# Layer 0's last query frequencies: two token groups in one call on eighths of TensorE

## The chip, the cores and the metric

One NeuronCore of a Trainium2 chip runs the whole network in one launch. The metric is the device time of the program in microseconds (us), the median of the runs shown. Engine names follow the profile: PE is TensorE's matmuls, PEld its weight loads, DVE is VectorE, ACT ScalarE, POOL GpSimd, SP the engine that issues most DMAs.

## The reference, cut to what matters

Four layers, each a gated cross-attention followed by a gated feed-forward part, on 4 x 256 tokens of width 256 with a context of 4 x 64 rows of width 64. The change concerns the cross-attention of layer 0 alone:

```python
q_hk = (hidden_q @ Wq.T).reshape(Bv, Sv, H, K)           # 16 heads
q_big = jnp.einsum('bshk,hkq->bshq', q_hk, w_kc_q)       # 192 values a head
q_big = _apply_rope(q_big, sin_q, cos_q)                 # rotation by position
kv_r = _apply_rope(kv_c, sin_k, cos_k)
q_r = jnp.einsum('bshq,hqr->bhsr', q_big, W_qr)
k_r = jnp.einsum('bld,hdr->bhlr', kv_r, W_kr)
scores = jnp.einsum('bhsr,bhlr->bhsl', q_r, k_r)
attn = jax.nn.softmax(scores, axis=-1)
ctx_c = jnp.einsum('bhsl,bld->bhsd', attn, kv_r)
```

The kernel folds `w_kc_q` into `Wq` and `W_kr` into `W_qr`, so that each head's rotated query of 192 values is multiplied by one matrix of 192 x 64 to the "latent" query of 64 values, which meets the rotated context directly. The rotation couples value q with value q + 96: a head has 96 frequencies, each with two sides.

## The kernel before, in words

The 1024 tokens are 8 tiles of 128 or two groups g of 512 (NG = 2). The 16 heads are taken four at a time, f = 0 to 3 (NQ = 4). Inside f, the heads are split by `up` (rows 0 to 63 or 64 to 127 of the partitions) and i (two heads in each half).

attention0 (L629 to L722) works on 24 rotations, step n. `rotated(n)` (L639) multiplies the folded query weights `weff0` with the transposed, normalised tokens xT[g] into a "wide" PSUM tile of 128 x 2 x 512 (s = 0, 1 are the two sides; each takes two accumulating matmuls through the helper on L389), multiplies it by the cosine and sine tables on VectorE (L650) and adds up on GpSimd (L658, L659). The result, `qr` or a slot of the ring `rotated`, holds for k = 0 and 1 the first 64 frequencies of head i = k, and for k = 2 the last 32 frequencies of both heads i of each half: four quarters of 32 rows, one head in each.

Steps before: unit u = 2 f + g, k = 0, 1, 2, so n = 3 u + k. `to_latent(u)` (L662, matmuls on L671) takes the results of k = 0 and 1 to latents: contraction over 64 rows, 64 output columns, accumulated over s in two PSUM tiles `mm` (one for each `up`), head i in the half of partitions 64 i to 64 i + 63. `rest_to_latent(u)` (L679, matmuls on L685) adds the result of k = 2: contraction over 64 rows that hold two heads, against a weight `rest` of 64 x 128 that is zero where a row's head is not the column's head. GpSimd sets `rest` to zero first (L457), and fold_scores0 (L450; matmuls on L470 and L484) fills the non-zero blocks. Then ScalarE copies both tiles into `qcT[g]` (L687).

What sets the order: each engine runs its own stream, and the loop on L693 places the calls: to_latent(u - 1) in step 3 u, rest_to_latent(u - 1) in step 3 u + 1, fold_queries0 for the next f (L504, matmuls on L516) in every sixth step, a piece of fold_output (L546) in four late steps, small preparations (`later`) from step 6. The layer norm of the second group and its transposes (L374) are called in step 1. The buffers: PSUM has four `mm` and two `wide` tiles; the SBUF pool `t4` has six slots, from which every rotation takes two (rope0, rope1) and every odd one a third (qr); even ones use the ring of two.

latent_attend (L578) follows. `values(b)` (matmuls on L591) makes the folded output weights for batch b, with index j for the head's half; `scores(t)` (L609) multiplies `qcT` with the block-diagonal context `bd_k`, whose two halves of rows are the two heads; softmax, transposes and the output product (L624) come behind. Groups are batches: g = 1 is b >= 2.

Of the kernel before, what the change touches and what calls it, by code (L numbers as in the profile page):

```python
# [38 lines left out]
B, S, D = 4, 256, 256  # L39
# [3 lines left out]
NG = T // TH  # L43
TPG = TH // P
L, DC = 64, 64
NH, DK, CQ, CQH, R = 16, 128, 192, 96, 64
NP = NH // 2
NQ = NH // 4
# [35 lines left out]
def tile_flamingo(ctx: ExitStack, tc: tile.TileContext, a: dict, out: bass.AP):  # L84
# [7 lines left out]
    def ps_mm():  # L92
        return psum.tile([P, 512], F32, tag="mm", name="mm", bufs=4)
# [356 lines left out]
    def fold_scores0():  # L450

        wqk = region("wqk", 2048, "wqk0")
        wide = wqk[:, :1024].rearrange("p (f i s d) -> p f i s d", f=NQ, i=2, s=2)
        rest = wqk[:, 1024:].rearrange("p (f s i d) -> p f s i d", f=NQ, s=2, i=2)
        nc.gpsimd.memset(rest, 0.0)  # L457
        rT = w_rk0[:, : NP * CQ].rearrange("r (h q) -> r h q", h=NP)
        kT = w_rk0[:, NP * CQ :].rearrange("r (h d) -> r h d", h=NP)
        for f2 in range(NQ // 2):  # L460
            wides = [ps_mm() for _ in range(2)]
            rests = [ps_mm() for _ in range(2)]
            for f in range(2):
                for i in range(2):
                    for s in range(2):
                        h = (f2 * 2 + f) * 2 + i
                        for up in range(2):
                            rows = slice(up * R, (up + 1) * R)
                            at_ = ((f * 2 + i) * 2 + s) * DC
                            nc.tensor.matmul(  # L470
                                wides[up][rows, at_ : at_ + DC],
                                rT[rows, h, s * 64 : (s + 1) * 64],
                                kT[rows, h, :],
                                start=True,
                                stop=True,
                            )
            for f in range(2):
                for i in range(2):
                    for s in range(2):
                        h = (f2 * 2 + f) * 2 + i  # L480
                        for up in range(2):
                            rows = slice(up * R, (up + 1) * R)
                            lo, at_ = up * R + i * 32, (f * 2 + s) * DC
                            nc.tensor.matmul(  # L484
                                rests[up][lo : lo + 32, at_ : at_ + DC],
                                rT[rows, h, 128 + s * 32 : 128 + (s + 1) * 32],
                                kT[rows, h, :],
                                start=True,
                                stop=True,
                                tile_position=(up * R, lo),  # L490
                            )
            fs = slice(f2 * 2, f2 * 2 + 2)
            for up in range(2):
                rows = slice(up * R, (up + 1) * R)
                evacuate(wide[rows, fs].rearrange("p f i s d -> p (f i s d)"), wides[up][rows])
                for i in range(2):
                    rows = slice(up * R + i * 32, up * R + (i + 1) * 32)
                    evacuate(
                        rest[rows, fs, :, i, :],
                        rests[up][rows, :256].rearrange("p (f s d) -> p f s d", f=2, s=2),  # L500
                    )
        return wide, rest.rearrange("p f s i d -> p f s (i d)")

    def fold_queries0(f):  # L504

# [69 lines left out]
        t = big[:, HALF:].rearrange("p (g r t) -> p g r t", g=NG, r=NP)  # L575
        return [t[:, g] for g in range(NG)]

    def latent_attend(qcT, wvo, gate):  # L578


        vos: dict = {}

        def values(b):

            v = region(("wqk", "weff")[b % 2], 2048, "vo").rearrange("p (q j o) -> p q j o", q=4, j=2)
            for r in range(2):
                pss = [ps_mm() for _ in range(2)]
                for a_ in range(2):
                    for j, ps in enumerate(pss):
                        rows = slice(j * DC, (j + 1) * DC)  # L590
                        nc.tensor.matmul(  # L591
                            ps[a_ * L : (a_ + 1) * L, :],
                            bd_k[rows, b, j * L : (j + 1) * L],
                            wvo[rows, 4 * r + a_ : 4 * r + a_ + 3 : 2, :],
                            start=True,
                            stop=True,
                        )
                for j, ps in enumerate(pss):
                    evacuate(v[:, 2 * r : 2 * r + 2, j, :], ps.rearrange("p (q o) -> p q o", q=2))
            vos[b] = v.rearrange("p q j o -> p (q j) o")  # L600

        def scores(t):
            g, i = divmod(t, TPG)
            if t % 2 == 0:
                values(t // 2)
            ps = ps_wide()
            for pr in range(NP):
                q, a_ = divmod(pr, 2)
                nc.tensor.matmul(  # L609
                    ps[:, q // 2, q % 2 * 256 : (q % 2 + 1) * 256].rearrange("p (j a l) -> p j a l", j=2, a=2)[:, :, a_, :],  # L610
                    qcT[g][:, pr, i * P : (i + 1) * P],
                    bd_k[:, t // 2, :],
                    start=True,
                    stop=True,
                )
            e = t4([P, NH, L], "attn")
            exponentials(e, ps.rearrange("p a (h l) -> p (a h) l", l=L))
            return e

        def attend(t, e):  # L620
            aT, vo = transposed_pairs(e), vos[t // 2]
            ps = ps_mm()
            for s in range(NP):
                nc.tensor.matmul(ps[:, :D], aT[:, s, :], vo[:, s, :], start=(s == 0), stop=(s == NP - 1))  # L624
            return ps

        in_flight(scores, attend, gate)

    def attention0(gate):  # L629

        xT = [transposed(layernorm(0))]
        fold_queries0(0)
        qcT = latents()
        ring = region("weff", 2048, "rotated").rearrange("p (i s t) -> p i s t", i=2, s=2)
        units = [(f, g) for f in range(NQ) for g in range(NG)]
        made: dict = {}
        sums: dict = {}

        def rotated(n):  # L639
            u, k = divmod(n, 3)  # L640
            f, g = units[u]
            ps = ps_wide()
            for s in range(2):
                mm2(ps[:, s, :], lambda c: weff0[:, c, f, 2 * k + s, :], xT[g])
# [14 lines left out]
            nc.gpsimd.tensor_tensor(qr[:, 1, :], halves[1][:, 0, :], halves[1][:, 1, :], ALU.add)  # L659
            made[n] = qr  # L660

        def to_latent(u):  # L662

            f, _ = units[u]
            pss = sums[u] = [ps_mm() for _ in range(2)]
            qrs = [made.pop(3 * u + i) for i in range(2)]
            for s in range(2):
                for i in range(2):
                    for up in range(2):
                        rows = slice(up * 64, (up + 1) * 64)  # L670
                        nc.tensor.matmul(  # L671
                            pss[up][i * DC : (i + 1) * DC, :],
                            wide[rows, f, i, s, :],
                            qrs[i][rows, s, :],
                            start=(s == 0),
                            stop=False,
                        )

        def rest_to_latent(u):  # L679
            f, g = units[u]  # L680
            pss, qr = sums.pop(u), made.pop(3 * u + 2)
            for s in range(2):
                for up in range(2):
                    rows = slice(up * 64, (up + 1) * 64)
                    nc.tensor.matmul(pss[up], rest[rows, f, s, :], qr[rows, s, :], start=False, stop=(s == 1))  # L685
            for up in range(2):
                last.append(nc.scalar.copy(qcT[g][:, 2 * f + up, :], pss[up]))  # L687

        wide = None
        later = prepare()  # L690
        last: list = []
        output = fold_output(w_kv0, [lambda: (w_o0, NH, lambda: None)])
        for n in range(3 * len(units) + 2):  # L693
            u, k = divmod(n, 3)
            if n == 1:
                xT.append(transposed(layernorm(1)))
            if u < len(units):
                rotated(n)
                if k == 1 and u % 2 == 0 and u // 2 + 1 < NQ:
                    fold_queries0(u // 2 + 1)  # L700
                if k == 1 and u >= len(units) - 4:
                    next(output)
            if wide is None:
                wide, rest = fold_scores0()
            if k == 0 and u >= 1:
                to_latent(u - 1)
            if k == 1 and u >= 1:
                rest_to_latent(u - 1)
            if n >= 6:
                next(later, None)  # L710
        tanh = nc.scalar.activation(tg, gates, AF.Tanh)
# [6 lines left out]
        wvo = at_once(output)  # L718
        for e in (0, 4, 8):
            load_experts0(e, e + 4)  # L720
        latent_attend(qcT, wvo, gate)
        load_experts0(12, 16)  # L722

    def fold1():
# [1030 lines left out]
```

## Time and profile before

| | us |
|---|---|
| median of 3 runs | 988.71 (983.85 to 992.39) |
| the profiled execution | 982.89 |
| its span, first to last instruction | 980.9 |
| PE busy in the span | 872.9 (4451 matmul records) |
| DVE, ACT, POOL busy | 531.6, 274.3, 300.0 |
| L389, 192 records | 88.8 |
| L671, 128 records in two groups | 15.5 and 15.5 |
| L685, 64 records in two groups | 8.2 and 7.9 |

A page of the profile shows, for one execution, groups of instructions: line, engine, operation, the names of what is written and read, the shape ("64*128" on PE: contraction rows by weight columns), the count, then busy time and mean ns of one, then the idle time of the engine just before them with what ended it. A group's busy time counts overlapped instructions once, so count times mean can be more. Other views give the chain of work that ended last in order of time, the busy time of all engines in a stretch, and who waited for whom. All times are from the span's start.

### The profile page before, as it was taken

What the parts mean: (1) busy time and instruction counts of PE and PEld (TensorE: products, weight loads), DVE (VectorE), ACT (ScalarE), POOL (GpSimd) and SP (SyncE); (2) the same over time, 40 slices, a digit from 0 to 9 for tenths busy, and PEclk for the clock granted to TensorE, in tenths of its full rate; (3) what the DMA queues carried; (4) which work ended last, traced back from release to release, by engine and by line L of the source; (5) the groups of instructions that cost most, each with busy time, mean ns of one, the idle gap of its engine ahead of it and who ended that gap; (6) DMA issues with size and microseconds to landing.
All of it is one profiled execution on the core that took longest, in us unless ns stands there. A gap on an engine that the chain in (4) does not pass through costs nothing.

```text
span 980.9 us, 12657 instructions
## 1 busy us (share of the span) xinstructions
PE 872.9 (89%) x4451; PEld 569.9 (58%) x4453; DVE 531.6 (54%) x1185; ACT 274.3 (28%) x531; POOL 300.0 (31%) x259
## 2 busy tenths in 40 slices
PE   5999998999899999997899978979638899999992
PEld 3544335876678866774547854746424556666661
DVE  4656455756953344552627749958785855222213
ACT  2211013334123232331223447034303532122220
POOL 1445451310065665751003128003101402133220
PEclk9999999999989999997999999979858989999997
DMA  9200017300154444225730000530000011011004
GB/s 351 84 15 11 28 36 230 89 22 22 33 153 160 131 152 151 90 69 157 260 115 1 1 1 27 189 116 2 22 0 1 1 44 33 22 48 39 29 16 140
DMA packets 35481, 75.82 MB, mean 77 GB/s; under 512 B 4551, under 2 KB 22207, under 8 KB 34106
## 3 DMA queue, kind: packets, MB, share of 16 engines
q1 hardware_dynamic: 27834, 56.22, 17.1%
q0 software_dynamic: 7296, 18.50, 6.1%
q8 instruction: 39, 0.64, 0.3%
q10 hardware_dynamic: 288, 0.26, 0.1%
q14 instruction: 24, 0.20, 0.1%
HBM read 63.42 MB, written 12.98 MB: 78 GB/s over the span
## 4 chain that ended last, share of the span: by engine, by line
PE 53%; DVE 17%; issue 14%; DMA 8%; POOL 4%; ACT 4%; SPq 0%; POOLq 0%; DVEq 0%; ACTq 0%
PE wide L389 9%; PE wide L1158 5%; PE mm L624 5%; DMA zz<-ring,scratch 4%; PE mm L1193 3%; PE wide L1400 3%; PE mm L419 2%; PE mm L1532 2%; POOL zz L1205 2%; PE mm L389 2%; PE wide L609 2%; PE mm L685 1%; PE mm L1421 1%; PE mm L897 1%; PE mm L671 1%
## 5 line engine op out<-in xcount | busy, mean ns | idle before, releaser
L405 POOL TENSOR_TENSOR attn<-attn,sm 128x1024 f32<-128x1024 f32 x32 | 60.8, 1900 | 235.1 <-DVE sm L404 163.1
L1178 DVE TENSOR_TENSOR blk<-wide,blk 128x176 f32<-128x176 f32 (+1 forms) x75 | 32.5, 433 | 142.0 <-ACT blk L1177 142.0
L650 DVE TENSOR_TENSOR rope<-wide,big 128x512 f32<-128x512 f32 x96 | 59.6, 683 | 57.1 <-PE wide L389 55.6
L389 PE MATMUL wide<-xT,big 128*128 128x512 f32 x192 | 88.8, 610 | 0.3 <-ACT big L524 0.3
L1129 POOL DMA_INDIRECT xs<-xd,big x55 | 55.3, 1005 | 70.3 <-DVE shared L1310 34.5
L1158 PE MATMUL wide<-big,blk 128*128 x220 | 74.1, 458 | 0.0
L1169 PE MATMUL wide<-big,blk 128*128 x160 | 72.2, 593 | 0.5 <-DVE blk L1143 0.5
L1205 POOL DMA_INDIRECT zz<-ring,big x55 | 56.1, 1021 | 31.9 <-DVE ring L1202 11.2
L389 PEld LDWEIGHTS wide<-xT,big 128*128 128x128 f32 x192 | 35.7, 193 | 48.7 <-issue 38.7
L1177 ACT ACTIVATE blk<-wide 128x176 f32<-128x176 f32 (+1 forms) x75 | 29.4, 392 | 122.8 <-PE wide L1158 61.6
L624 PE MATMUL mm<-vo,attnT 128*128 128x256 f32 x256 | 60.4, 390 | 0.9 <-ACT attnT L420 0.9
L1193 PE MATMUL mm<-big,blk 88*128 x220 | 56.8, 379 | 0.5 <-ACT blk L1186 0.5
L624 PEld LDWEIGHTS mm<-vo,attnT 128*128 128x128 f32 x256 | 48.4, 194 | 9.5 <-ACT attnT L420 3.3
L420 ACT COPY attnT<-mm 128x512 f32<-128x512 f32 x64 | 35.0, 588 | 65.0 <-PE mm L419 65.0
L374 PE MATMUL mm<-ident,xn 128*128 128x128 f32 x112 | 24.3, 363 | 30.3 <-DVE xn L362 18.0
L1193 PEld LDWEIGHTS mm<-big,blk 88*128 88x128 f32 x220 | 41.4, 189 | 15.5 <-ACT blk L1186 1.4
L1158 PEld LDWEIGHTS wide<-big,blk 128*128 128x128 f32 x220 | 39.5, 190 | 12.5
L403 DVE TENSOR_REDUCE sm<-attn 128x16 f32<-128x1024 f32 x32 | 38.9, 1215 | 14.5 <-ACT attn L397 12.3
L419 PE MATMUL mm<-ident,attn 128*128 128x128 f32 x256 | 36.3, 289 | 10.8 <-POOL attn L405 10.8
L1169 PEld LDWEIGHTS wide<-big,blk 128*128 128x128 f32 x160 | 28.8, 190 | 28.9 <-issue 28.2
L424 DVE SCALAR_TENSOR_TENSOR x<-mm,tg,x 128x256 f32<-128x256 f32 x48 | 22.9, 476 | 39.8 <-PE mm L624 19.7
L1129 POOL DMA_INDIRECT xs<-xd,scratch x20 | 19.2, 961 | 81.5 <-PE mm L1141 59.5
(334 smaller groups left out, 1702.4 us busy)
## 6 DMA issues: line engine op xcount, KB each, us to landing
big<-in_L_w_gate_up SPq DMA_DIRECT2D x8, 1024.0 KB, 8.2
zt<-zz SPq DMA_DIRECT2D x16, 384.0 KB, 5.1
big<-in_L_w SPq DMA_DIRECT2D x4, 1408.0 KB, 6.8
big<-in_L_w_down SPq DMA_DIRECT2D x8, 512.0 KB, 11.9
w_L_qk<-in_L_qk SPq DMA_DIRECT2D x4, 896.0 KB, 8.6
big<-in_L_w SPq DMA_DIRECT2D x4, 704.0 KB
big<-in_L_wo SPq DMA_DIRECT2D x1, 2048.0 KB, 12.8
xd<-xn SPq DMA_DIRECT2D x16, 128.0 KB, 1.8
```

Of the source, the lines that this page charges most:

```text
L389: nc.tensor.matmul(ps, w(c), xT[:, c, :], start=(c == 0), stop=(c == 1))
L403: nc.vector.tensor_reduce(sm, e, AX.X, ALU.add)
L405: nc.gpsimd.tensor_tensor(e, e, sm.unsqueeze(2).to_broadcast([P, groups, n]), ALU.mult)
L419: nc.tensor.transpose(ps[:, i * P : (i + 1) * P], ev[:, pr * P : (pr + 1) * P], ident)
L420: nc.scalar.copy(aT[:, half * 4 : half * 4 + 4, :].rearrange("p i t -> p (i t)"), ps)
L624: nc.tensor.matmul(ps[:, :D], aT[:, s, :], vo[:, s, :], start=(s == 0), stop=(s == NP - 1))
L650: nc.vector.tensor_tensor(m[:, s, :].rearrange("q (b t) -> q b t", t=S), ps[:, s, :].rearrange("q (b t) -> q b t", t=S), table, ALU.mult,)
L1129: nc.gpsimd.indirect_dma_start(out=xs, out_offset=None, in_=self.xd, in_offset=bass.IndirectOffsetOnAxis(ap=self.gather[:, b : b + 1].bitc ...
L1158: nc.tensor.matmul(ps[:, 0, : 2 * n], st[:, c * P : (c + 1) * P], self.w[:, bass.ds(r + c * 2 * n, 2 * n)], start=False, stop=(c == 1),)
L1169: nc.tensor.matmul(ps[:, k, :n], st[:, c * P : (c + 1) * P], self.w[:, bass.ds(r + (2 * c + k) * n, n)], start=(c == 0), stop=(c == 1),)
L1193: nc.tensor.matmul(ps[:, :D], hT[:, j * P : (j + 1) * P], self.w[: self.chunk, bass.ds(r + j * D, D)], start=(j == 0), stop=(j == self.n - 1),
L1205: s = nc.gpsimd.indirect_dma_start(out=self.z, out_offset=bass.IndirectOffsetOnAxis(ap=self.scatter[:, b : b + 1].bitcast(U32), axis=0), i ...
```

## The change

- `rest` loses its zero blocks and the memset: a weight of 32 rows by 64 columns for each quarter of rows.
- The order of rotations inside f becomes (k, g) = (0,0), (1,0), (2,0), (2,1), (0,1), (1,1), so that the two results of k = 2 stand side by side; n = 6 f + m.
- `rest_to_latent(f)` is called once for each f, in its sixth step, for both groups: 16 matmuls on tiles of 32 x 64 with a written tile position. For g = 0 it closes the sums that to_latent(f, 0) opened in the fourth step; for g = 1 it opens them, and to_latent(f, 1) closes them in the second step of the next f.
- For g = 1 the two heads of a pair lie in swapped halves (`half = i ^ g`), and values() for batches 2 and 3 stores its output with j swapped to match.
- `finished` does the copies of L687, two for each f and g as before.
- The layer norm and transposes of the second group are called in step 2 in place of step 1.

```diff
@@ -453,8 +453,7 @@

         wqk = region("wqk", 2048, "wqk0")
         wide = wqk[:, :1024].rearrange("p (f i s d) -> p f i s d", f=NQ, i=2, s=2)
-        rest = wqk[:, 1024:].rearrange("p (f s i d) -> p f s i d", f=NQ, s=2, i=2)
-        nc.gpsimd.memset(rest, 0.0)
+        rest = wqk[:, 1024:1536].rearrange("p (f s d) -> p f s d", f=NQ, s=2)
         rT = w_rk0[:, : NP * CQ].rearrange("r (h q) -> r h q", h=NP)
         kT = w_rk0[:, NP * CQ :].rearrange("r (h d) -> r h d", h=NP)
         for f2 in range(NQ // 2):
@@ -496,10 +495,10 @@
                 for i in range(2):
                     rows = slice(up * R + i * 32, up * R + (i + 1) * 32)
                     evacuate(
-                        rest[rows, fs, :, i, :],
+                        rest[rows, fs],
                         rests[up][rows, :256].rearrange("p (f s d) -> p f s d", f=2, s=2),
                     )
-        return wide, rest.rearrange("p f s i d -> p f s (i d)")
+        return wide, rest

     def fold_queries0(f):

@@ -575,7 +574,7 @@
         t = big[:, HALF:].rearrange("p (g r t) -> p g r t", g=NG, r=NP)
         return [t[:, g] for g in range(NG)]

-    def latent_attend(qcT, wvo, gate):
+    def latent_attend(qcT, wvo, gate, swapped=False):


         vos: dict = {}
@@ -596,7 +595,7 @@
                             stop=True,
                         )
                 for j, ps in enumerate(pss):
-                    evacuate(v[:, 2 * r : 2 * r + 2, j, :], ps.rearrange("p (q o) -> p q o", q=2))
+                    evacuate(v[:, 2 * r : 2 * r + 2, (1 - j) if swapped and b >= B // 2 else j, :], ps.rearrange("p (q o) -> p q o", q=2))
             vos[b] = v.rearrange("p q j o -> p (q j) o")

         def scores(t):
@@ -628,17 +627,18 @@

     def attention0(gate):

+
         xT = [transposed(layernorm(0))]
         fold_queries0(0)
         qcT = latents()
         ring = region("weff", 2048, "rotated").rearrange("p (i s t) -> p i s t", i=2, s=2)
-        units = [(f, g) for f in range(NQ) for g in range(NG)]
+        turns = [(0, 0), (1, 0), (2, 0), (2, 1), (0, 1), (1, 1)]
         made: dict = {}
         sums: dict = {}

         def rotated(n):
-            u, k = divmod(n, 3)
-            f, g = units[u]
+            f, m = divmod(n, 6)
+            k, g = turns[m]
             ps = ps_wide()
             for s in range(2):
                 mm2(ps[:, s, :], lambda c: weff0[:, c, f, 2 * k + s, :], xT[g])
@@ -659,53 +659,72 @@
             nc.gpsimd.tensor_tensor(qr[:, 1, :], halves[1][:, 0, :], halves[1][:, 1, :], ALU.add)
             made[n] = qr

-        def to_latent(u):
-
-            f, _ = units[u]
-            pss = sums[u] = [ps_mm() for _ in range(2)]
-            qrs = [made.pop(3 * u + i) for i in range(2)]
+        def to_latent(f, g):
+
+            if not g:
+                sums[f, g] = [ps_mm() for _ in range(2)]
+            pss = sums[f, g]
+            qrs = [made.pop(6 * f + 4 * g + i) for i in range(2)]
             for s in range(2):
                 for i in range(2):
+                    half = i ^ g
                     for up in range(2):
                         rows = slice(up * 64, (up + 1) * 64)
                         nc.tensor.matmul(
-                            pss[up][i * DC : (i + 1) * DC, :],
+                            pss[up][half * DC : (half + 1) * DC, :],
                             wide[rows, f, i, s, :],
                             qrs[i][rows, s, :],
-                            start=(s == 0),
-                            stop=False,
+                            start=(s == 0 and g == 0),
+                            stop=(s == 1 and g == 1),
                         )
-
-        def rest_to_latent(u):
-            f, g = units[u]
-            pss, qr = sums.pop(u), made.pop(3 * u + 2)
+            if g:
+                finished(f, g)
+
+        def rest_to_latent(f):
+
+            sums[f, 1] = [ps_mm() for _ in range(2)]
+            qrs = [made.pop(6 * f + 2 + g) for g in range(NG)]
             for s in range(2):
-                for up in range(2):
-                    rows = slice(up * 64, (up + 1) * 64)
-                    nc.tensor.matmul(pss[up], rest[rows, f, s, :], qr[rows, s, :], start=False, stop=(s == 1))
-            for up in range(2):
-                last.append(nc.scalar.copy(qcT[g][:, 2 * f + up, :], pss[up]))
+                for g in range(NG):
+                    for i in range(2):
+                        for up in range(2):
+                            lo, half = up * 64 + i * 32, i ^ g
+                            nc.tensor.matmul(
+                                sums[f, g][up][half * DC : (half + 1) * DC, :],
+                                rest[lo : lo + 32, f, s, :],
+                                qrs[g][lo : lo + 32, s, :],
+                                start=(s == 0 and g == 1),
+                                stop=(s == 1 and g == 0),
+                                tile_position=(lo, half * DC),
+                            )
+            finished(f, 0)
+
+        def finished(f, g):
+            for up, ps in enumerate(sums.pop((f, g))):
+                last.append(nc.scalar.copy(qcT[g][:, 2 * f + up, :], ps))

         wide = None
         later = prepare()
         last: list = []
         output = fold_output(w_kv0, [lambda: (w_o0, NH, lambda: None)])
-        for n in range(3 * len(units) + 2):
-            u, k = divmod(n, 3)
-            if n == 1:
+        for n in range(6 * NQ + 2):
+            f, m = divmod(n, 6)
+            if n == 2:
                 xT.append(transposed(layernorm(1)))
-            if u < len(units):
+            if f < NQ:
                 rotated(n)
-                if k == 1 and u % 2 == 0 and u // 2 + 1 < NQ:
-                    fold_queries0(u // 2 + 1)
-                if k == 1 and u >= len(units) - 4:
+                if m == 1 and f + 1 < NQ:
+                    fold_queries0(f + 1)
+                if m % 3 == 1 and f >= NQ - 2:
                     next(output)
             if wide is None:
                 wide, rest = fold_scores0()
-            if k == 0 and u >= 1:
-                to_latent(u - 1)
-            if k == 1 and u >= 1:
-                rest_to_latent(u - 1)
+            if m == 3 and f < NQ:
+                to_latent(f, 0)
+            if m == 5:
+                rest_to_latent(f)
+            if m == 1 and f >= 1:
+                to_latent(f - 1, 1)
             if n >= 6:
                 next(later, None)
         tanh = nc.scalar.activation(tg, gates, AF.Tanh)
@@ -718,7 +737,7 @@
         wvo = at_once(output)
         for e in (0, 4, 8):
             load_experts0(e, e + 4)
-        latent_attend(qcT, wvo, gate)
+        latent_attend(qcT, wvo, gate, swapped=True)
         load_experts0(12, 16)

     def fold1():
```

## The prediction

> **What bounds the kernel now.** I read the page's slices first (TensorE is the busiest engine, 872.9 us of a 980.9 us span), then the waits and busy times of the stage that the diff touches, then its chain in order of time. The stage of attention0 runs from the first matmul on L389 at 16.80 us to the last on L685 at 154.73 us. The busy times of its middle (columns: window, length, busy and count on PE, PEld, DVE, ACT, POOL, clock, DMA share, GB/s):
>
> ```profile
> 34.00:149.50 115.50, 115.50 (x421) 48.34 (x423) 61.52 (x101) 14.73 (x36) 54.56 (x45) 1.00 0.12 34
> ```
>
> TensorE is busy in all 115.50 us, at full clock; VectorE is at 53%, GpSimd at 47%, DMA at 0.12. So TensorE's own sequence is the stage's length, and a matmul taken from it should shorten the kernel. The chain, from one call of to_latent to the same call two units later (columns: start, length, what):
>
> ```profile
> 40.89 1.88 PE mm L671 x16
> 42.77 3.63 PE wide L389 x8
> 46.40 1.92 PE mm L685 x8
> 48.31 7.06 PE wide L389 x16
> 55.38 1.88 PE mm L671 x16
> 57.26 3.63 PE wide L389 x8
> 60.89 2.85 PE mm L516 x16
> 63.73 1.92 PE mm L685 x8
> ```
>
> It is unbroken PE. Each block has a fixed part: 8 matmuls of L389 take 3.63 us, 16 take 7.06, so 8 more cost 3.43 and a block carries about 0.19 us besides. One record is one slot of 3.43 / 8 = 0.43 us. The trace has two records for each matmul of the source (192 on L389 for 96).
>
> Next, how many records share a slot. L671 has 16 in 1.88 us, four slots and the block's part, hence four side by side; L685 has 8 in 1.92 us, four slots, two side by side. Their sizes are 64x64 and 64x128:
>
> ```profile
> L671 PE MATMUL mm<-rotated,wqk 64*64 64x512 f32 x64 | 15.5, 602 | 0.0
> L671 PE MATMUL mm<-qr,wqk 64*64 64x512 f32 x64 | 15.5, 602 | 0.0
> L685 PE MATMUL mm<-qr,wqk 64*128 64x512 f32 x32 | 8.2, 622 | 1.1 <-POOL qr L658 1.0
> L685 PE MATMUL mm<-rotated,wqk 64*128 64x512 f32 x32 | 7.9, 615 | 0.0
> ```
>
> A slot costs the same with one tile (L389), two (L685) or four (L671). On L685 half of the multiplications are with zeros that the memset on L457 wrote: each quarter of the rows serves one head, yet all 128 columns are swept. The end of the stage:
>
> ```profile
> 149.60 1.30 DVE rope L650 x2
> 150.90 0.02 issue
> 150.92 0.04 POOLq L658
> 150.96 0.09 issue
> 151.06 1.27 POOL qr L658
> 152.32 1.23 POOL qr L659
> 153.56 0.04 issue
> 153.60 1.13 PE mm L685 x4
> 154.73 2.24 PE mm L591 x16
> ```
>
> Here TensorE waits: the last rotation goes through VectorE and GpSimd before its matmuls.
>
> **What the Trainium skill says.** "TensorEngine Tiling (Array Packing)", section Tiling Modes, lists 32x64 tiles: eight independent ones, and says that changing the mode drains TensorE; the 0.19 us per block agrees. Its section Restrictions and Gotchas says that different row tiles may not access one PSUM bank at once. L671 and L685 fit: their two row tiles write two banks. In the new order this bears on the case, see below. "TensorE: Matmul & The Clock Gate", section Part 3 (Packing small matmuls), gives 3.07x for four row tiles and 10.6x for sixteen tiles at 512 columns[...]. The trace before has no 32-row tile and no more than four at once, so eight are not shown here.
>
> **The change part by part.**
>
> 1. The rest's matmuls. Before, per f: two calls (g = 0, 1), each 2 s x 2 halves = 4 matmuls, 8 records, 1.92 us: 3.84. After, one call of 2 s x 2 g x 2 heads x 2 halves = 16 matmuls, 32 records, on eight distinct 32x64 tiles (four row quarters by two column halves). If eight go side by side it is 32 / 8 = 4 slots, so 1.92 us, as before but for both groups. Bounds: eight side by side at best (1.92), one at a time at worst (32 x 0.43 = 13.8). I take 1.92. Reasons: the slot did not grow from one to two to four tiles; within one column half the four row quarters write four different banks (that is what the head swap of g = 1 brings about: half = i ^ g), so the skill's rule is met wherever outputs meet; each row quarter is read by two column halves, as on L671 already. Issue is fast enough: L484 has 32 records of 64x32 tiles in 0.60 us on the chain, 19 ns each, and here 0.43 / 8 = 54 ns each is needed.
>
> 2. Blocks. Before, six rotations (two units) were broken by four calls; after by three (to_latent of g = 0 behind the fourth rotation, the rest behind the sixth, to_latent of g = 1 behind the second of the next f). Two blocks of L389 merge into one: 0.19 us per f. Saving per f: 1.92 + 0.19 = 2.11 us. Check on the chain: two units without the extra folds take 2 x 1.88 + 2 x 3.63 + 2 x 1.92 + 2 x 7.06 = 28.98 us; after, 3 x 7.06 + 2 x 1.88 + 1.92 = 26.86.
>
> 3. The end. Before the end of the last rotation lie 14 calls (7 to_latent, 7 rests) before the change and 10 after (7 and 3): 4 x 2.11 = 8.44 us. Then the order turns: the last rest (1.92 us, its inputs long made) fills the place of the last to_latent (1.88), and the last to_latent waits for the same GpSimd operation, its second half needing 2 slots as L685's did (1.13 us on the chain). So the tail stays: 0.0.
>
> 4. The removed memset on GpSimd (L457, 0.94 us): its engine sat idle 21.2 us before its first rotation. Nothing. The copies of rest out of PSUM keep count and size; the swapped index in values() keeps count and size of every copy. Nothing, in both cases because the work is the same.
>
> 5. The copies to qcT (L687, 0.54 us each, 16 before and after) now come behind the rest and behind the second to_latent. At the sixth rotation all four "mm" banks are held for the time of the rest and two copies (1.92 + 1.07 us). The next request for one is fold_queries0 or fold_output two rotations later (7.06 us), which covers it; the fold of queries finds two free banks, as before. Uncovered it would cost 1.07 us per f.
>
> 6. The rotated tiles live two or three rotations, as before; the ring slot written in step n was freed in step n-1 or n-3. Inputs are made (5 us through VectorE and GpSimd) two rotations (7.06 us) ahead of each call, as before. VectorE's 16.3 us and GpSimd's 15.3 per f (24 x 0.68; 12 x 1.28) stay below TensorE's 26.9.
>
> 7. layernorm(1) moves from the second step to the third. In the trace it ran on VectorE at 13.47 to 18.12 us, ahead of the first rotation's multiplications at 22.24 though the source has it behind them: it went when x had landed and the engine was free. No DMA is issued in the moved step. I take 0. Were it bound to its new place, it would start behind the second rotation's multiplications: 4 x (0.40 + 0.18) + 0.30 + 0.18 + 4 x 0.35 = 4.2 us, then the transposes; TensorE has only the fold of queries (2.76 us) meanwhile, so it would lose some 4 us with what surrounds it.
>
> Sum: -8.4 us. Profiled execution: span 980.9, its time 982.89 (2.0 lies around it): to 974.4. It was below the median of the runs shown (988.71, from 983.85 to 992.39); on that, 988.7 - 8.4 = 980.3 us. Behind the stage everything hangs on its end: the experts' loads are issued when its inputs are done (145.00 us), and no DMA wait stands on the chain until 359.83 us, so the gain is not swallowed.
>
> **Rivals.**
> - *Four side by side, not eight.* The two quarters of one 64-row half write the same bank (in different column halves); if that serialises, the rest takes 8 slots: 8 x 0.43 + 0.2 = 3.64 us against 3.84, and with the merged block 0.39 us per f is saved: -1.6 us, 987.1. For: no trace line shows two row tiles in one bank. Against: [...]they lie on different partitions.
> - *Two side by side (slower).* If a matmul with 32 rows blocks the array for its neighbours in the same 64 rows and columns, a rest takes 16 slots: 7.08 us against 3.84 + 0.19, +3.05 per f, +12.2 us: 1000.9. It decides from 3.6 side by side: 32 x 0.43 / 3.6 + 0.2 = 4.03. Against: L671.
> - *The moved layernorm stalls the start:* -8.4 + 4 = -4.4 us, 984.3. Against: its place in the trace.
> - *Doing other than it says:* the order of later stages may come out differently, since the trace's order is not the source's. A few us of either sign; no line argues for it.
>
> **How the numbers follow.** Forecast 0.75 (980.3, its own range 975 to 986: runs spread 8.5 us); four side by side 0.08; slower rival 0.05; stalled start 0.07; reordering 0.05. The range 972 to 988 leaves out the slower rival and the outer parts of the others. A change of 1% (9.9 us) is about what a measurement of this kernel can tell from none. The forecast's -0.85% lies just within it: of its 0.75 I give 0.31 to over 1% faster and 0.44 to within; the other cases add 0.03 faster, 0.15 within, 0.07 slower.
>
> **What would show it.** The new line of the rest: 32 records of 32x64 in some 1.9 us, four calls; starts eight to a slot. Three blocks of 7.06 us per f; the first matmul of values() some 8.4 us before 154.73. Wrong: 3.6 us or more per rest, TensorE idle between 25 and 40 us, or a gain at the stage's end that is gone by the end of the span.

## The result and the profile after

| | before | after |
|---|---|---|
| median of 20 runs, us | 988.73 (983.72 to 993.63) | 980.85 (977.70 to 988.27) |
| ratio of the runs | | 0.9935, 95% interval 0.9917 to 0.9953 |
| span of the profiled execution, us | 980.9 | 978.1 |

The changed kernel is faster by 0.65% (0.47 to 0.83%), some 6.4 us; the forecast was 0.85%, 980.3 us. The two medians lie 7.9 us apart, further than the ratio says; runs of one kernel spread over some 10 us, and the ratio with its interval is what is used below. In e2_no_swap below, two of the 22 executions took 2252 and 3065 us in a slow state and are left out of its ratio.

The new rest in the list of instruction groups of the changed kernel (L692 is the matmul of rest_to_latent, L673 that of to_latent, L590 that of values(), L608 that of scores(), L515 that of fold_queries0 and L545 that of fold_output):

```profile
L692 PE MATMUL mm<-qr,wqk 32*64 32x512 f32 x64 | 7.8, 600 | 0.0
L692 PE MATMUL mm<-rotated,wqk 32*64 32x512 f32 x64 | 7.8, 600 | 0.0
```

There are 128 records in place of 64, and 7.8 us of busy time for each name. The two lines are the two token groups' halves of the same four calls, so they overlap almost wholly in time, while those of L685 did not. How the eight tiles start is seen in the timeline of one call (columns: start of the first, length until the last ends, engine, line, instruction, names, shape, count):

```profile
50.70 0.66 PE L692 MATMUL mm<-rotated,wqk 32*64 32x512 f32 x4
50.72 0.66 PE L692 MATMUL mm<-qr,wqk 32*64 32x512 f32 x4
51.18 0.61 PE L692 MATMUL mm<-rotated,wqk 32*64 32x512 f32 x4
51.20 0.61 PE L692 MATMUL mm<-qr,wqk 32*64 32x512 f32 x4
```

Eight records start within 0.05 us, the next eight one slot later. The chain of the changed kernel, in order of time, over six rotations:

```profile
41.82 1.88 PE mm L673 x16
43.70 7.06 PE wide L389 x16
50.77 1.90 PE mm L692 x32
52.67 7.06 PE wide L389 x16
59.73 2.85 PE mm L515 x16
62.58 1.88 PE mm L673 x16
```

A call of 32 records takes 1.90 us, where a call of 8 took 1.92. One after another, at the prediction's slot of 0.43 us, 32 records would take 13.8 us by estimate, 7.2 times as long. TensorE still has no gap in the middle of the stage (the windows' columns are those of the prediction), and it still runs at full clock:

```profile
34.95:142.30 107.35, 107.35 (x465) 45.42 (x464) 62.34 (x101) 13.31 (x33) 53.64 (x44) 1.00 0.12 31
```

The end of the stage in the chain:

```profile
134.04 3.63 PE wide L389 x8
137.67 1.01 PE mm L545 x8
138.69 3.65 PE wide L389 x8
...
142.42 1.30 DVE rope L650 x2
...
143.88 1.27 POOL qr L658
145.16 1.24 POOL qr L659
146.39 0.04 issue
146.44 0.65 PE mm L673 x2
147.08 0.03 PE mm L590 x2
147.12 0.40 PE mm L673 x2
147.51 2.24 PE mm L590 x14
149.75 2.00 PE wide L608 x16
```

It is the wait of before, with another call behind it. The first lines show something new: a piece of fold_output (L545) stands alone between two rotations and cuts their block in two.

**Where the span went.** In the chain of the kernel before, the first matmuls of scores(), which end the stage, stand at:

```profile
156.97 2.00 PE wide L609 x16
```

The stage measured by itself, from the start of the first record of to_latent to that of the first of scores(), fell from 116.08 us (40.82 to 156.90) to 107.93 us (41.76 to 149.68, rounded); the chain's lines start 0.07 us later at both ends. That is 8.15 us, yet the spans differ by 2.8. The other 5.4 us are lost outside of the stage: to_latent began 0.94 us later, and from the first scores to the end it took 828.4 us in place of 824.0. The order of instructions on every engine is the same behind the stage in both kernels; only two neighbouring loads of the experts' weights on SP, issued at the end of the stage, have changed places. So those 4.4 us are either a property of these two executions or an effect of timing; the experiments below tell.

### The profile page after: what moved, and what is told of

It reads as the page before. It is cut to its first block, busy times and chain, and to the rows that moved or that the text cites. A ratio compares the mean times of both kernels' runs of the same rounds, so it can differ in the third digit from the quotient of the medians.

```text
span 978.1 us, 12784 instructions
## 1 busy us (share of the span) xinstructions
PE 868.7 (89%) x4517; PEld 566.9 (58%) x4517; DVE 532.5 (54%) x1185; ACT 273.9 (28%) x531; POOL 299.1 (31%) x258
## 4 chain that ended last, share of the span: by engine, by line
PE 53%; DVE 17%; issue 14%; DMA 7%; POOL 4%; ACT 4%; SPq 0%; POOLq 0%; DVEq 0%; ACTq 0%
PE wide L389 9%; PE wide L1177 5%; PE mm L623 5%; DMA zz<-ring,scratch 4%; PE mm L1212 3%; PE wide L1419 3%; PE mm L419 2%; POOL zz L1224 2%; PE mm L1551 2%; PE mm L389 2%; PE mm L673 1%; PE wide L608 1%; PE mm L1440 1%; PE mm L916 1%; PE mm L1279 1%
## 5 line engine op out<-in xcount | busy, mean ns | idle before, releaser
L389 PEld LDWEIGHTS wide<-xT,big 128*128 128x128 f32 x192 | 36.0, 194 | 47.5 <-issue 41.9
L1162 DVE COPY blk<-mm 128x256 f32<-128x256 f32 x75 | 31.3, 419 | 24.3 <-PE mm L1160 17.9
```

The costliest lines, as they stand in the source:

```text
L389: nc.tensor.matmul(ps, w(c), xT[:, c, :], start=(c == 0), stop=(c == 1))
```

## The experiments

All ratios are to the kernel before on the same chip; its median was 988.73 us beside the changed kernel, 980.83 beside e1 to e4 and 981.49 beside e5 to e7. A ratio rests on 5 to 22 executions, a stage on one profile. "Stage" is the time from the first record of to_latent to the first of scores(), "behind" the time from there to the end, both read from the starts in the trace.

| kernel | stage, us | behind, us | ratio, 95% interval |
|---|---|---|---|
| before | 116.08 | 824.0 | 1 |
| changed | 107.93 | 828.4 | 0.9935 (0.9917 to 0.9953) |
| e1_ln_back | 107.92 | 828.9 | 0.9916 (0.9887 to 0.9945) |
| e2_no_swap | 113.32 | 826.5 | 0.9983 (0.9965 to 1.0001) |
| e3_quarters_alone | 115.76 | 824.0 | 1.0006 (0.9982 to 1.0030) |
| e4_rest_doubled | 113.42 | 822.8 | 0.9984 (0.9969 to 1.0000) |
| e5_tail_and_folds | 107.16 | 824.2 | 0.9911 (0.9885 to 0.9937) |
| e6_rest_left_out | 96.86 (see there) | 856.4 | 1.0153 (1.0125 to 1.0180) |
| e7_changed_again | 107.92 | 823.7 | 0.9936 (0.9917 to 0.9954) |

**e1_ln_back: the layer norm back in step 1.**

```diff
-            if n == 2:
+            if n == 1:
                 xT.append(transposed(layernorm(1)))
```

> The changed kernel with one edit undone: the second group's layer norm and transposes are called in step 1 again. My theory (the gain comes from the merged rests alone): the stage ends as in the changed kernel, within 0.3 us, and the time is that of the changed kernel, 0.9935 of the kernel before within the interval. The rival that the moved call brings part of the gain: the stage ends 1 to 4 us later. The rival that the moved call costs something: it ends 1 to 4 us earlier.

The stage takes 107.92 us, the changed kernel's within 0.01. It ended 3.2 us earlier, though, at 146.51 us against 149.68, and by the wording of the expectation that speaks for a cost of the move. But the difference lies ahead of the stage, in the first rotation and the landing of x: from the second rotation's first matmul to to_latent, where the transposes stand, it is 15.81 us here and 15.85 in the changed kernel. And e2 and e4, which keep the moved call, reach to_latent as early, at 37.54 and 38.85 us, where e1 does at 38.59. The move is worth nothing that can be seen.

**e2_no_swap: the same instructions on four tiles.**

```diff
-                            lo, half = up * 64 + i * 32, i ^ g
+                            lo, half = up * 64 + i * 32, i
...
-                    half = i ^ g
+                    half = i
...
-        latent_attend(qcT, wvo, gate, swapped=True)
+        latent_attend(qcT, wvo, gate)
```

> The changed kernel without the head swap: both groups put head i into half i, so a call of the rest has 32 records on only four different 32x64 tiles. Same order of all instructions. My theory (eight different tiles run side by side, a slot is 0.43 us): 8 slots in place of 4, each rest 3.6 us in place of 1.9, +1.72 us each; the last is mostly hidden in the wait for the last rotation, so the stage ends 5.2 to 5.9 us later than in the changed kernel, some 2.4 us before that of the kernel before; ratio to before 0.997 to 0.999. The rival that the array runs only four 32-row tiles at once in any case: no difference from the changed kernel.

The chain of this kernel:

```profile
39.49 7.06 PE wide L389 x16
46.55 3.59 PE mm L692 x32
50.14 7.06 PE wide L389 x16
```

A rest takes 3.59 us in place of 1.90 for 32 records of the same shape, in the same order, and the stage is longer by 5.39 us, within the 5.2 to 5.9 expected. What the swap buys is that the second group's heads land on the four tiles that the first group's leave idle. The rival that only four 32-row tiles run at once is gone.

**e3_quarters_alone: the zeros left out, the groups apart.** The weight loses its zero blocks and the memset as in the change (not shown here); the matmuls become:

```diff
...
-                for up in range(2):
-                    rows = slice(up * 64, (up + 1) * 64)
-                    nc.tensor.matmul(pss[up], rest[rows, f, s, :], qr[rows, s, :], start=False, stop=(s == 1))
+                for i in range(2):
+                    for up in range(2):
+                        lo = up * 64 + i * 32
+                        nc.tensor.matmul(
+                            pss[up][i * DC : (i + 1) * DC, :],
+                            rest[lo : lo + 32, f, s, :],
+                            qr[lo : lo + 32, s, :],
+                            start=False,
+                            stop=(s == 1),
+                            tile_position=(lo, i * DC),
+                        )
```

> The kernel before with the zero blocks gone and nothing else of the change: each rest stays in its place for one group, on four tiles of 32x64 (16 records) in place of two of 64x128 (8 records); two row quarters write one PSUM bank in different column halves. My theory (what pays is that two groups share the slots, not that the zeros are left out): 4 slots before and after, each rest 1.9 us, the stage ends within 0.3 us of the kernel before, ratio 1.000. The rival that two quarters in one bank serialise: 3.6 us a rest, +1.72 us times 7 or 8, 12 to 14 us later, ratio 1.013. The rival that leaving out the zeros is itself the gain: some 7 us earlier.

The chain of this kernel:

```profile
43.82 3.63 PE wide L389 x8
47.45 1.88 PE mm L685 x16
49.32 7.06 PE wide L389 x16
```

The stage is 0.32 us shorter, a hair beyond the 0.3 expected: eight calls at 1.88 in place of 1.92 us. The ratio is 1 within its interval. Leaving out the multiplications with zeros frees half of the array and gains nothing as long as nothing runs there. It also answers the prediction's rival on PSUM: here two row quarters write one bank at once, in different column halves (their records start 7 ns apart and last 0.59 us), and 16 records on four tiles still take four slots.

**e4_rest_doubled: twice the rest.**

```diff
-            for s in range(2):
+            for s, again in ((0, 0), (0, 1), (1, 0), (1, 1)):
                 for g in range(NG):
...
-                                start=(s == 0 and g == 1),
-                                stop=(s == 1 and g == 0),
+                                start=(s == 0 and g == 1 and not again),
+                                stop=(s == 1 and g == 0 and again == 1),
```

> The changed kernel with every matmul of the rest issued twice (the sums then hold the last 32 frequencies' part twice, so another function is computed): 64 records a call in place of 32, on the same eight tiles. My theory: +4 slots, +1.72 us for each of the first three calls and mostly hidden for the last: the stage ends 5.2 to 5.9 us later than in the changed kernel and the time rises by as much, ratio to before 0.997 to 0.999. If what follows the stage swallows a change of its end, the time rises by 3 us or less although the stage ends 5 us later. If the eight tiles did not share slots, each call would rise by more than 3 us.

The chain of this kernel:

```profile
47.86 3.62 PE mm L692 x64
51.48 7.06 PE wide L389 x16
```

64 records in 3.62 us: 1.72 us for another 32, four slots of eight. The stage is 5.49 us longer than the changed kernel's. The last call is mostly hidden, as expected: three calls make 5.16 us. The ratio moved from 0.9935 to 0.9984, 0.0049 of 988.7 us or 4.8 us, with some 2.4 us of uncertainty from the two intervals. So most of a change of this size comes through to the end, and no part of it is seen to be swallowed.

**e5_tail_and_folds: two small edits more.**

```diff
+            adder = nc.vector if n == 6 * NQ - 1 else nc.gpsimd
-            nc.gpsimd.tensor_tensor(qr[:, 1, :], halves[1][:, 0, :], halves[1][:, 1, :], ALU.add)
+            adder.tensor_tensor(qr[:, 1, :], halves[1][:, 0, :], halves[1][:, 1, :], ALU.add)
...
-                if m % 3 == 1 and f >= NQ - 2:
+                if m in (1, 3) and f >= NQ - 2:
```

> The changed kernel with two small edits that its trace suggests: the pieces of fold_output stand in the second and fourth step of f = 2 and 3, where a call of to_latent breaks the rotations anyway (two of them stood alone between rotations and cost a block's 0.19 us each), and the last rotation's addition goes to VectorE in place of GpSimd (0.6 us behind its last multiplication in place of 1.27 us behind GpSimd's subtraction). My theory of blocks and of the tail: from the first to_latent to the first scores 0.9 to 1.3 us less than in the changed kernel (107.9 us), 106.6 to 107.0; in the time 0.1%, too little to tell. If blocks cost nothing and the tail hangs on something else: 107.9.

The chain of this kernel at its end:

```profile
130.84 1.01 PE mm L545 x8
131.86 1.88 PE mm L674 x16
133.74 7.06 PE wide L389 x16
140.80 1.90 PE mm L693 x32
142.70 2.49 PE mm L674 x14
145.19 0.06 PE mm L590 x2
145.25 0.37 PE mm L674 x2
145.62 2.24 PE mm L590 x14
```

The stage is 107.16 us, 0.77 less; 0.9 to 1.3 were expected, so this missed. The blocks gave what was expected (0.40 us up to the last rotation, two times 0.19). The tail gave 0.38, less than the 0.5 or more that was left for it: VectorE and GpSimd are off the chain now, and what stands there is TensorE's own work. The ratio is the lowest of all, and its interval overlaps that of the changed kernel.

**e6_rest_left_out: no rest at all.**

```diff
-                            start=(s == 0 and g == 0),
-                            stop=(s == 1 and g == 1),
+                            start=(s == 0),
+                            stop=(s == 1),
...
-            qrs = [made.pop(6 * f + 2 + g) for g in range(NG)]
-            for s in range(2):
-                for g in range(NG):
...
+            for g in range(NG):
+                made.pop(6 * f + 2 + g)
```

> The changed kernel without the rest's matmuls (the last 32 frequencies are left out of the latents; their rotations are still made). Four calls of 1.90 us go; the first three leave the path with their block's 0.19 us, 3 x 2.09 = 6.3 us; the fourth filled the wait for the last rotation. With fewer PSUM banks held, six matmuls of values() move ahead of the last to_latent, into that wait: up to 1.7 us more. From the first to_latent to the first scores 99.9 to 101.6 us against 107.9, and the time falls by as much against the changed kernel: ratio to the kernel before 0.985 to 0.988 if what follows keeps the gain, 0.993 if what follows swallows it.

The time rose by 1.5% with less work, which neither theory allowed. Three things were not foreseen. First, the stage's mark moved: scores() of the first tile, which needs only the first group, now runs ahead of the last to_latent, so 96.86 us is no fair reading. Up to the start of the last rotation's last matmul, to_latent's part took 94.47 us against 99.97 in the changed kernel: 5.50 us less where 6.3 were expected. Second, TensorE's sequence now has a gap, which makes up for the difference (columns as before, with the idle time ahead of the line and what ended it):

```profile
81.97 2.38 PE L389 MATMUL wide<-xT,big 128*128 128x512 f32 x5 [0.76 <-DVE rope L650]
```

VectorE is late there: between its multiplications it also prepares the biases of layer 0's experts, whose load has just landed. In the changed kernel the same work lies off the chain. So with the rests gone, VectorE is the next limit in this place. To the first gather of layer 0's experts it is 213.7 us (40.26 to 254.0) against 219.7 (40.04 to 259.7) in e7 and 218.0 in the first profile of the changed kernel: 4.3 to 6.0 us less. Third, other latents send tokens to other experts. The same group of the expert stages, first of this kernel and then of the changed one:

```profile
L1185 DVE TENSOR_TENSOR blk<-wide,blk 128x176 f32<-128x176 f32 (+1 forms) x78 | 34.6, 444 | 150.3 <-ACT blk L1184 150.1
```

```profile
L1197 DVE TENSOR_TENSOR blk<-wide,blk 128x176 f32<-128x176 f32 (+1 forms) x75 | 32.5, 434 | 143.5 <-ACT blk L1196 139.8
```

78 blocks of tokens in place of 75: layer 3 makes 23 gathers in place of 20, and its part from the first gather to the end takes 189.1 us in place of 161.3 (changed). Those 28 us hide the gain of the stage. The run shows the price of the rests in the stage, less the gap, and nothing on the total.

**e7_changed_again: the changed kernel once more.**

> The changed kernel once more, on the chip of the two others. My theory: what the profile of the changed kernel lost behind the stage (828.4 us from the first scores to the end, against 824.0 before) belongs to that one execution, so this one shows 822 to 829 us there, the stage from the first to_latent to the first scores is 107.9 us again, and the ratio to the kernel before is 0.992 to 0.994 (8.15 us of stage are 0.83%). If the changed kernel's later stages are slower by 4 us of their own, it shows 828 us or more there and a ratio of 0.995 or more.

Stage 107.92, behind 823.7, ratio 0.9936: the second reading agrees with the first, and the 4.4 us that the first profile lost behind the stage are absent. The time behind is 822.8 to 828.9 us over the kernels with the changed order (e6 apart), and 824.0 in both profiles with the order of before (before, e3). The loss of the first profile lies in layer 0's expert blocks. Between the same two halts of TensorE around them it took 185.7 us (257.6 to 443.3), and 179.6 to 181.7 us in the other eight profiles. Longer halts inside the blocks explain only a part of it: 1.69 us at 393.9 and 1.54 us at 406.5, where five of the other profiles have one of 1.40 to 2.13 us and three have none. What causes the loss wasn't settled. Up to the experts the gain of the stage is whole: from the first to_latent to the first gather it takes 227.8 us before, and 218.0, 219.6 and 219.6 us in the changed kernel, e1 and e7.

## Why the prediction was right, point by point

- *TensorE's sequence is the stage's length.* Right: no gap before or after, and the stage followed each change of that sequence (e2, e4, e5).
- *1. The rest's matmuls, 1.92 us for 32 records.* Right: 1.90 measured. The reasons held too: the slot does not grow up to eight tiles, and with four tiles for the same 32 records (e2) it is 3.59.
- *2. Blocks, 0.19 us per f.* Right in mechanism; e5 measured it on another pair of blocks (0.40 us for two). The count was off: the pieces of fold_output, which had stood next to a rest, now stand twice alone between rotations and give back 0.4 us. What the 0.19 us consist of, a drain as the prediction suggests or something else, no run separates. The prediction looked at the order of the calls and not at what else lay beside the removed ones.
- *3. The end, 0.0.* Right: from the start of the last rotation's last matmul to the first scores 8.00 us before and 7.96 after.
- *4 and 6.* The memset and the buffers: no wait for either is in the profile after. *5.* The copies: ACT waits for the rest (L704, 61.7 us in all), and TensorE's chain never waits for them; only two weight loads of values() do, for 1.0 us together and off the chain. A copy takes 0.59 us; the prediction's 0.54 is the busy time divided by the count, which is smaller because neighbours overlap, and nothing hangs on it.
- *7. layernorm(1), 0.* Right, shown by e1; it still runs ahead of the first rotation (from 13.77 us, as soon as x lands).
- *The sum.* 8.44 us were forecast for the stage and 8.15 measured: the two lone pieces took 0.40, and calls shorter by 0.02 and the end by 0.04 gave 0.10 back.
- *The total.* 980.3 us were forecast and 980.85 measured; that these medians agree so closely is in part luck. By the ratios the gain was measured twice at 6.4 us (0.9935 and 0.9936), and 8.15 us of stage alone would be 0.9918, at the edge of both intervals. Worked out in the same way from its stage, every ratio of the table but e1's (and e6's, which does other work) lies above this estimate, by 0.0002 to 0.0019, each inside its interval or at the edge. So the runs suggest a loss of 1 to 2 us outside of the stage, but don't show it, and its place and cause are open: e3, with the order of before, lies 0.0009 above its estimate too, and one profile a kernel, with 6 us of spread behind the stage, can't settle it. That the order of later stages might change was given as a rival; apart from the two neighbouring loads it did not, and what these two do to the time was not tested.
- *The rivals.* Four side by side and two side by side are excluded by the timeline and by e2 against the changed kernel; PSUM banks by e3; the stalled start by e1 and by the chain of the changed kernel, which is TensorE's work alone from 25 us to the end of the last rotation. On PSUM the prediction had only an argument, that the outputs lie on different partitions, and no trace of before showed it. It held, and the rule on row tiles and banks that the prediction cites is broader than what is measured here: two row tiles share a bank at no cost when they write different column halves. The same partitions of one bank were not tried.

## What to carry to other kernels

Where a TensorE stage has no gap, count slots and not multiplications: here the zeros cost nothing as long as nothing else ran in their place (e3), and with something to run there the place was worth a whole call. To fill it, bring two users into one step and give the second the tiles that the first leaves idle, here by swapping which half holds which head and undoing that in a later index. When calls are merged, look at what stood beside the removed ones, and judge a change of under 1% by the stage in the trace, since the start (4.3 us of spread here) and the later stages (6.1 us) differ from one execution to the next by as much as the change is worth.

## What the runs showed of the hardware beyond what was expected

- The first rotation's eight matmul records took 5.40 us on the chain before and 5.55 in the changed kernel, but 3.72 in e1 and 3.73 in e2, with the same work: the granted clock in that stretch was 0.68 before and 1.00 in e1 and e2. Together with the landing of x, this made the first to_latent begin at 37.5 to 41.9 us over the nine profiles, a spread of half the gain of the stage.
- Two row tiles can write one PSUM bank at once at no cost if they use different column halves (e3: 16 records on four 32x64 tiles in 1.88 us, where two 64x128 tiles in two banks took 1.92).
- Eight 32x64 tiles run side by side: in fp32 at 512 columns 32 records take 1.90 us on eight tiles and 3.59 on four (e2), and 64 take 3.62 on eight (e4).
